# Two-layer graph network on one core: list places dropped and weighted on ScalarE after layer 0, and more room before the last steps

## The chip, the cores and the metric

The kernel runs on one core of one Trainium2 chip. The core has five engines that run side by side, each on its own queue of instructions in a fixed order: TensorE (PE, with its weight loads PEld), VectorE (DVE), ScalarE (ACT), GpSimd (POOL) and SyncE (SP, which here only issues DMAs). They meet through semaphores. The metric is the device time of one execution in microseconds (us); less is better.

## What is computed

Sixteen graphs of 1024 nodes with 64 channels each go through two layers. Layer 0 is a dense, degree-normalised neighbour sum of a normalised input. Layer 1 takes, for every node and channel, a weighted sum of three quantiles over the node's neighbours, after some neighbours have been removed, and puts the result through a two-layer MLP.

```python
def reference(x, adj, nodemask, W1, b1, W2, b2):
    h = relu(layernorm(x))                                  # layer 0
    x = x + matmul(adj / clip(sum(adj, 2), 1), h)
    h = relu(layernorm(x))                                  # layer 1
    valid = dilate_adj(adj, nodemask) > 0                   # with the node itself
    agg = 0
    for tau, wt in ((.25, .25), (.5, .5), (.75, .25)):
        agg += wt * quantile(h over the valid neighbours, tau)   # linear interpolation
    y = relu((h + agg) @ W1 + b1) @ W2 + b2
    return x + y * nodemask

def dilate_adj(adj, mask):
    # a node with m > 10 neighbours removes each (m+1)//2-th of them; an edge that
    # either end removes is gone
    ...
```

The adjacency matrices are sparse (a few hundred neighbours for the first nodes of a graph, a handful for most), so layer 1 works on lists of neighbours.

## The kernel before

**Layer 0** goes graph by graph. SP loads 128 rows of adjacency at a time (`at`); PE transposes them and multiplies them with the normalised input; ScalarE takes signs, VectorE turns the signs into lists of neighbour numbers (`rec`). At the end of a graph its normalised rows go to a table in DRAM (`tab`), and POOL scatters a row per node (`srt<-row`) into one of four sorted tables, one for each group of four graphs, so that nodes with lists of similar length stand together.

**Layer 1** works on jobs (class `Job`, from line 797). A job takes T blocks of 128 nodes whose lists have at most n-1 places. There are ten jobs of short lists for each of the four groups (`gat`, up to 15 places), and four jobs of long lists (88, 31, 24 and 20 places, tiles with an l in front). Before a group's jobs run, `group` (line 1027) prepares them: `recs` and `nodes_i` are made, POOL reads one block of adjacency rows (`gat_rows`), two corrections are scattered to the table (`tab<-drop`). `long_lists` (line 1145) prepares a long list in the same way, with a read of adjacency rows into `lat`. Of a job:

- `run` (808): POOL gathers, one indirect DMA for each place and block, from the table into `places` (four buffers) or `lplaces`. A last wait (831) hands over to VectorE.
- `sort` (844): VectorE finds which places have been removed (`rem`, `gone`), how many are left (`ok`, `valid`), the quantile positions (`q`) and three weights for each place (`wu`, finished by ScalarE). It adds a huge number to the places that are gone (876 to 880). Then come the steps of a sorting network between `places` and `other` (in PSUM) or `long_other`; the weights are added up (`w`) and multiplied with the sorted places into `prod`, or in place for a long list (938 to 946).
- `layers` (965): PE adds up and transposes, ScalarE copies (`ot`), PE multiplies, ScalarE applies the relu (`hid`), PE multiplies, VectorE adds the residual (`y`, 1013), and POOL scatters the T blocks of y to the output (`out_dram`, 1022).

**What sets the order.** The kernel is written as streams (Python generators) that a planner, class `Plan`, merges. A stream yields the engine that it needs next, a function for the time at which its operands are ready or a buffer is free, and sometimes a rank. The planner keeps a clock for each engine by prices that stand in the code, always continues the stream that can begin first, and at equal times the one of lower rank. The order in which VectorE and POOL execute is the order in which the planner emitted their instructions; at run time an engine stands before its next instruction until that one's semaphores are there, and everything behind it stands too. `at(tile)` is the planned time at which a tile is ready, `room(name, bufs)` the planned time at which the oldest of so many buffers is free. The constants SLACK and LOOSE (lines 213 and 214) are planned microseconds added to `at`, so that an instruction is placed somewhat after its operands are planned to be ready. `later` (837) gives the rank of a job's steps: ahead of others while POOL has few gathers left to issue (`progress["ahead"] < AHEAD`), behind them otherwise. `progress["batches"] == B` means that layer 0 of all sixteen graphs has been emitted.

Of the kernel before, what the change touches and what calls it, by code (L numbers as in the profile page):

```python
# [9 lines left out]
F32 = mybir.dt.float32  # L10
BF = mybir.dt.bfloat16
# [3 lines left out]
AF = mybir.ActivationFunctionType  # L15
# [196 lines left out]
AHEAD = 16  # L212
SLACK = 2.0
LOOSE = 7.0


class Timed:
# [146 lines left out]
def list_path(ctx, tc, x, adj, nodemask, w1, b1, w2, b2, out, go):  # L364
# [434 lines left out]
    class Job:  # L799
# [8 lines left out]
        def run(self):  # L808
            n, T, pool, short = self.n, self.T, self.pool, self.short

            since = []
            own = () if short else (lambda rank: self.rank,)
            pace = lambda: since[0] + 1.3 * len(since) if not short else 0.0
            yield "POOL", lambda: max(
                at(self.idx), room(self.name, self.bufs), room("S", 4) if short else 0.0
            ), *own
            A = self.A = new(pool, [P, n, T, W], F32, self.name, self.bufs, users=1)
            progress["ahead"] += T * (n - 1)
            if short:
                mine = self.S  # L820
                self.S = new(pool, [P, T, C], F32, "S", 4, users=1)
                nc.sync.dma_start(self.S, mine[:, :, :C])
                self.residual = mine[:, :, X1:R0]
            for t in range(T):
                for k in range(n - 1):
                    if t or k:
                        yield "POOL", pace, *own
                    since.append(since[0] if since else plan.clock["POOL"])
                    gather(A[:, k + 1, t, :], self.table, self.idx[:, t, k:k + 1])
                    progress["ahead"] -= 1  # L830
            yield "DVE", lambda: max(
                at(A, self.S) + SLACK, room("prod", 2) if short else 0.0,
                room("other" if short else "long_other", 1),
            ), self.later
            yield from self.sort()

        def later(self, rank):

            return rank - 900 if progress["ahead"] < AHEAD else rank + 2000

        def urgent(self):
            return -1000 if progress["ahead"] < AHEAD else 5000

        def sort(self):
# [5 lines left out]
                rem, A[:, 1:, :, C:],  # L850
                self.node.unsqueeze(1).unsqueeze(3).to_broadcast([P, n - 1, T, 2]), OP.is_equal,
            )
            gone = new(pool, [P, n - 1, T], F32, name + "gone", bufs)
            nc.vector.tensor_tensor(gone, rem[:, :, :, 0], rem[:, :, :, 1], OP.max)
            ok = new(pool, [P, n - 1, T], F32, name + "ok", bufs)
            nc.vector.scalar_tensor_tensor(
# [10 lines left out]
                q, taus.unsqueeze(2).to_broadcast([P, K, T]),  # L867
                valid.unsqueeze(1).to_broadcast([P, K, T]), OP.mult,
            )
            u = new(pool, [P, K, count, T], F32, name + "wu", 1)  # L870
            nc.vector.tensor_tensor(
                u, col_f[:, :count].unsqueeze(1).unsqueeze(3).to_broadcast([P, K, count, T]),
                q.unsqueeze(2).to_broadcast([P, K, count, T]), OP.subtract,
            )
            vals = A[:, 1:, :, :].rearrange("p k t w -> p (k t) w")[:, :, :C]
            nc.vector.scalar_tensor_tensor(
                vals,
                gone.rearrange("p k t -> p (k t)").unsqueeze(2).to_broadcast([P, (n - 1) * T, C]),
                HUGE, vals, op0=OP.mult, op1=OP.add,
            )  # L880
            if short:
                Bt = new(ps_o, [P, 3 * HALF], F32, "other", 1, users=1)
                other = Bt[:, :n * T * C].rearrange("p (k t c) -> p k t c", k=n, t=T)
            else:
                other = Bt = new(pool, [P, n, T, C], F32, "long_other", 1, users=1)
            yield "ACT", lambda: at(u) + SLACK
            nc.scalar.activation(u, u, AF.Abs)
            nc.scalar.activation(u, u, AF.Relu, bias=wt0, scale=-QUANTILES[0][1])

            def places(copy, run, shift=0):  # L890
                first, d1, n1, d2, n2 = run
# [36 lines left out]
            w = new(pool, [P, count, T], F32, name + "w", bufs)  # L928
            nc.vector.tensor_tensor(w, u[:, 0, :, :], u[:, 1, :, :], OP.add)
            nc.vector.scalar_tensor_tensor(w, u[:, 2, :, :], 2.0, w, op0=OP.mult, op1=OP.add)  # L930

            total = max(count + 1, 4)
            prod = None
            if short:
                prod = new(pool, [P, T, total, C], F32, "prod", 2, users=1)
                if count + 1 < total:
                    nc.vector.memset(prod[:, :, count + 1:, :], 0.0)
            for copy in range(2):
                for run in runs_of([k for k in range(count) if copies[k] == copy]):
                    first, step, number = run[:3]  # L940
                    sl = slice(first, first + step * (number - 1) + 1, step)
                    src = places(copy, run)
                    nc.vector.tensor_tensor(
                        prod[:, :, sl, :].rearrange("p t k c -> p k t c") if short else src, src,
                        w[:, sl, :].unsqueeze(3).to_broadcast([P, number, T, C]), OP.mult,
                    )
            if short:
                free(A)
                free(Bt)
                yield "ACT", lambda: at(S)  # L950
                nc.scalar.copy(prod[:, :, count, :], S[:, :, :C])
                free(S)

                terms = [
                    [prod[:, t, k:min(k + 2, total), :].rearrange("p k c -> p (k c)")
                     for k in (0, *range(4, total, 2), 2)]
                    for t in range(T)
                ]
                plan.add(self.layers(terms, [prod]), self.urgent)
            else:  # L960
                terms = [[places(copies[k], (k, 1, 1, 1, 1))[:, 0, 0, :] for k in range(count)]
                         + [S[:, 0, :C]]]
                plan.add(self.layers(terms, [A, Bt]), -1000)

        def layers(self, terms, sources):

            T, R = self.T, terms[0][0].shape[1]
            yield "PE", lambda: max(at(*sources) + LOOSE, room("y", 5), room("pt", 2))
            y = new(mlp, [P, T, CO], F32, "y", 5, users=1)
            x1 = y  # L970
            if self.short:
                nc.sync.dma_start(x1, self.residual)
# [2 lines left out]
            for t0 in range(0, T, 4):  # L975
                ts = range(t0, min(t0 + 4, T))
                M = len(ts) * P
                if t0:
                    yield "PE", lambda: room("pt", 2)
                pt = new(ps_t, [P, HALF], F32, "pt", 2, users=1)  # L980
                for i, t in enumerate(ts):
                    for k, term in enumerate(terms[t]):
                        nc.tensor.matmul(
                            pt[:term.shape[1], i * P:(i + 1) * P], term, ident,
                            start=(k == 0), stop=(k == len(terms[t]) - 1),
                        )
                if t0 + 4 >= T:
                    for tile_ in sources:
                        free(tile_)
                yield "ACT", lambda: max(at(pt) + SLACK, room("ot", 2))  # L990
                ot = new(mlp, [2 * C, HALF], F32, "ot", 2)
                nc.scalar.copy(ot[:R, :M], pt[:R, :M])
                free(pt)
                yield "PE", lambda: max(at(ot) + SLACK, room("ps_small", 3))
                ph = new(ps_s, [P, HALF], F32, "ps_small", 3, users=1)
                nc.tensor.matmul(ph[:, :M], w1_sb[:R, :], ot[:R, :M], start=True, stop=True)
                yield "ACT", lambda: max(at(ph) + SLACK, room("hid", 2))
                hid = new(mlp, [H, HALF], F32, "hid", 2)
                nc.scalar.activation(hid[:, :M], ph[:, :M], AF.Relu, bias=b1_sb)
                free(ph)  # L1000
                yield "PE", lambda: max(at(hid) + SLACK, room("ps_small", 3))
                py = new(ps_s, [P, HALF], F32, "ps_small", 3, users=1)
                pv = py[:, :len(ts) * CO].rearrange("p (t c) -> p t c", c=CO)
                nc.tensor.matmul(
                    py[:, :len(ts) * CO], ones_f[:1, :], b2_sb[:, :len(ts) * CO],
                    start=True, stop=False,
                )
                for i, t in enumerate(ts):
                    nc.tensor.matmul(
                        pv[:, i, :], hid[:, i * P:(i + 1) * P], w2_sb, start=False,  # L1010
                        stop=(i == len(ts) - 1),
                    )
                yield "DVE", lambda: at(py) + LOOSE
                for i, t in enumerate(ts):
                    nc.vector.scalar_tensor_tensor(
                        y[:, t, :], pv[:, i, :], self.mask[:, t:t + 1], x1[:, t, :],
                        op0=OP.mult, op1=OP.add,
                    )
                free(py)

            for t in range(T):
                yield "POOL", lambda: at(y) + LOOSE
                scatter(out_rows, y[:, t, :], self.nodes_i[:, t:t + 1], scatters)
            free(y)
            progress["jobs"][self.g] += 1
# [1 line left out]
    def group(g):  # L1027
# [22 lines left out]
        gather(full, adj_rows, nodes_i[:, 0:1])  # L1050
        yield "DVE", always

        found = new(grp, [P, NTAU, 8 * NSEG], BF, "gfound", 1)
        nc.vector.tensor_scalar(found, lists, 0.0, None, op0=OP.is_gt)
        m = tiny.tile([P, NTAU], F32, name="gm")
        nc.vector.tensor_reduce(m, found, AX.X, OP.add)
# [52 lines left out]
        nc.vector.scalar_tensor_tensor(  # L1109
            full, col_f, node[:, 0:1], full, op0=OP.not_equal, op1=OP.mult  # L1110
        )
        nb = new(grp, [P, N], BF, "nb", 1)
        nc.vector.tensor_scalar(nb, full, 0.0, None, op0=OP.is_gt)
        cum = full
        nc.vector.tensor_tensor_scan(cum, nb, zeros, 0.0, op0=OP.add, op1=OP.add)
# [421 lines left out]
```

## Time and profile before

| | |
|---|---|
| median of 3 runs | 1572.41 us (1570.78 to 1575.34) |
| profiled execution | 1573.65 us, its span 1571.9 us |
| mean granted TensorE clock in it | 0.687 |
| last row scatter of layer 0 begins | 826.16 us |
| last gather begins | 1537.34 us |
| last store of y begins | 1563.06 us |

The page cuts the span into 40 slices; a digit is the busy share of a slice in tenths:

```profile
DVE  6767899997997699999556897659779889878962
ACT  7889888346565536664630000000000010000001
POOL 0222238665578767568676666587777678566775
```

Layer 0 ends a little after the middle. Behind it ScalarE has almost nothing to do, while VectorE sorts and POOL gathers. All instructions that the planner records carry line 225, that of its helper, so groups are told apart by their tiles: `places<-tab,idx` is a gather, `out_dram<-y,nodes_i` a store, `places<-gone,places` the addition that drops places, `prod<-places,w` a product with weights. These rows have places (p) x elements, the count, the busy time, the mean of one in ns and the idle time before it:

```profile
L225 POOL DMA_INDIRECT places<-tab,idx x496 | 507.4, 1023 | 159.9 <-issue 146.1
L225 POOL DMA_INDIRECT lplaces<-tab,lidx x163 | 173.7, 1066 | 51.0 <-issue 47.9
L225 POOL DMA_INDIRECT out_dram<-y,nodes_i x124 | 130.6, 1053 | 99.2 <-DVE y L225 53.6
L225 DVE SCALAR_TENSOR_TENSOR y<-ps_small,recs,y 128x64 f32<-128x64 f32 x124 | 28.0, 276 | 81.0 <-PE ps_small L225 80.9
```

"issue" is time in which the engine waited for nothing that the profile shows.

### The profile page before, as it was taken

The page shows a single profiled execution, that of the slowest core. Times are in us where ns is not written, and L with a number is a line of the kernel's source. Part 1 is how long each engine was busy: PE and PEld are TensorE (multiplying, and loading weights), DVE is VectorE, ACT ScalarE, POOL GpSimd, SP SyncE. Part 2 cuts the span into 40 slices and gives each one's busy share as a digit, 9 for nine tenths or more (in the row PEclk, how much of TensorE's full clock was granted, in tenths as well). Part 3 has the DMA queues.
Part 4 walks back from the last instruction along what each step waited for, and adds up shares of the span by engine and source line. Part 5 has one row for each costly group of instructions (what it writes and reads, how often), then busy time and mean ns, then how long its engine had stood idle before and what let it go on. Part 6 is the DMA issues. An engine that isn't in the chain of part 4 may idle for free. (4 is left out here: it accounts for less than half of the span.)

```text
span 1571.9 us, 14933 instructions
## 1 busy us (share of the span) xinstructions
PE 744.4 (47%) x3192; PEld 465.3 (30%) x3192; DVE 1260.4 (80%) x4174; ACT 578.5 (37%) x1746; POOL 989.3 (63%) x1149
## 2 busy tenths in 40 slices
PE   5787776365756754855880001200021367124355
PEld 2334443133343532532450001100021156023244
DVE  6767899997997699999556897659779889878962
ACT  7889888346565536664630000000000010000001
POOL 0222238665578767568676666587777678566775
PEclk8888998686977866976895555555555567555657
DMA  5455666244542433652222111111121111111110
GB/s 161 134 149 167 175 198 188 71 124 100 177 121 60 120 106 108 165 149 66 75 51 66 41 38 36 33 27 23 25 41 34 24 28 24 28 31 36 31 29 21
DMA packets 135530, 128.95 MB, mean 82 GB/s; under 512 B 100696, under 2 KB 103384, under 8 KB 135432
## 3 DMA queue, kind: packets, MB, share of 16 engines
q1 hardware_dynamic: 102696, 86.46, 19.7%
q0 software_dynamic: 32736, 41.47, 11.6%
q8 instruction: 27, 0.44, 0.1%
q14 instruction: 71, 0.58, 0.1%
HBM read 108.57 MB, written 19.28 MB: 81 GB/s over the span
## 5 line engine op out<-in xcount | busy, mean ns | idle before, releaser
L225 POOL DMA_INDIRECT places<-tab,idx x496 | 507.4, 1023 | 159.9 <-issue 146.1
L225 PE MATMUL pt<-ident,prod 128*128 128x128 f32 (+1 forms) x736 | 168.0, 395 | 627.5 <-DVE prod L225 586.7
L225 PEld LDWEIGHTS pt<-ident,prod 128*128 128x128 f32 (+1 forms) x736 | 136.6, 273 | 659.6 <-DVE prod L225 406.0
L225 PE MATMUL ps_small<-att,h 128*65 128x512 f32 x512 | 260.1, 657 | 44.1 <-ACT h L225 28.3
L225 POOL DMA_INDIRECT srt<-row,to x128 | 129.5, 1012 | 176.2 <-ACT row L225 154.8
L225 POOL DMA_INDIRECT lplaces<-tab,lidx x163 | 173.7, 1066 | 51.0 <-issue 47.9
L225 PE MATMUL pt<-ident,at 128*128 128x128 f32 x1024 | 167.3, 308 | 80.7 <-ACT att L225 68.9
L225 POOL DMA_INDIRECT out_dram<-y,nodes_i x124 | 130.6, 1053 | 99.2 <-DVE y L225 53.6
L225 DVE MAX8 rec<-sg 128x8 f16<-128x256 f16 x512 | 180.1, 414 | 4.4
L225 PEld LDWEIGHTS pt<-ident,at 128*128 128x128 f32 x1024 | 129.4, 157 | 126.2 <-ACT att L225 93.7
L225 ACT ACTIVATE sg<-at 128x1024 f16<-128x1024 f32 x128 | 134.9, 1054 | 54.2 <-DMA at<-in_adj_dram 34.6
L225 ACT COPY att<-pt 128x512 f32<-128x512 f32 x256 | 141.5, 582 | 22.7 <-PE pt L225 20.7
L225 ACT COPY ot<-pt 128x128 f32<-128x128 f32 (+3 forms) x56 | 22.2, 401 | 308.9 <-PE pt L225 308.6
L225 ACT ACTIVATE wu<-wu 128x39 f32<-128x39 f32 (+9 forms) x40 | 9.4, 235 | 337.7 <-DVE wu L225 337.6
L225 PEld LDWEIGHTS ps_small<-att,h 128*65 128x65 f32 x512 | 75.8, 154 | 184.3 <-issue 128.5
L225 DVE TENSOR_TENSOR sg<-sg,keyed 128x1024 f16<-128x1024 f16 x128 | 87.6, 684 | 37.3 <-ACT sg L225 37.2
L225 DVE SCALAR_TENSOR_TENSOR y<-ps_small,recs,y 128x64 f32<-128x64 f32 x124 | 28.0, 276 | 81.0 <-PE ps_small L225 80.9
L225 DVE TENSOR_TENSOR other<-places,other 128x64 f32<-128x64 f32 (+6 forms) x204 | 69.7, 342 | 5.6
L225 DVE TENSOR_TENSOR places<-places,other 128x64 f32<-128x64 f32 (+2 forms) x208 | 62.4, 309 | 4.9
L225 DVE TENSOR_TENSOR long_other<-lplaces 128x512 f32<-128x512 f32 (+5 forms) x124 | 63.9, 553 | 0.4
L225 DVE TENSOR_TENSOR lplaces<-long_other 128x512 f32<-128x512 f32 (+7 forms) x116 | 61.4, 567 | 0.1
L225 DVE TENSOR_TENSOR places<-other,places 128x128 f32<-128x128 f32 (+5 forms) x160 | 54.9, 343 | 3.5
(206 smaller groups left out, 1516.1 us busy)
## 6 DMA issues: line engine op xcount, KB each, us to landing
at<-in_adj_dram SPq DMA_DIRECT2D x128, 512.0 KB
places<-tab,idx POOLq DMA_INDIRECT x496
tab<-row SPq DMA_DIRECT2D x16, 264.0 KB
xt<-in_x_dram SPq DMA_DIRECT2D x16, 256.0 KB
lplaces<-tab,lidx POOLq DMA_INDIRECT x163
recs<-srt SPq DMA_DIRECT2D x4, 544.0 KB
srt<-row,to POOLq DMA_INDIRECT x128
out_dram<-y,nodes_i POOLq DMA_INDIRECT x124
```

What stands on the lines that cost most here:

```text
L225: ins = getattr(self._engine, op)(*args, **kwargs)
```

## The change

Five things are changed, all in the planner's streams:

1. For a job whose preparation is emitted once layer 0 is done, the huge number is no longer added by one VectorE instruction: ScalarE multiplies `gone` by it and adds it as a per-partition bias, one activation for each place and block.
2. For such a job ScalarE also multiplies with the weights, one activation for each place and block: for a short list those places whose sorted value ends in `places` (copy 0), for a long list all.
3. The preparation up to `wu` is separated from the sort. It waits for its operands and for the buffers of `gone` and `wu` (two of each for short lists), by a rank of its own (`soon`); the sort then waits for the places, for `prod` and for `other`.
4. y is placed LATE = 14 instead of LOOSE = 7 planned microseconds after its matmuls, the store 14 instead of 7 after y, and y has six buffers instead of five.
5. In `group`, `found` and `nb` share a buffer.

```diff
+LATE = 14.0
...
             yield "DVE", lambda: max(
-                at(A, self.S) + SLACK, room("prod", 2) if short else 0.0,
-                room("other" if short else "long_other", 1),
-            ), self.later
+                at(A, self.S) + SLACK,
+                *(room(("" if short else "l") + name, 2 if short else 1) for name in ("gone", "wu")),
+            ), self.soon
             yield from self.sort()
...
+        def soon(self, rank):
+
+            return rank - (950 if progress["ahead"] < AHEAD else -1900)
...
-            vals = A[:, 1:, :, :].rearrange("p k t w -> p (k t) w")[:, :, :C]
-            nc.vector.scalar_tensor_tensor(
-                vals,
-                gone.rearrange("p k t -> p (k t)").unsqueeze(2).to_broadcast([P, (n - 1) * T, C]),
-                HUGE, vals, op0=OP.mult, op1=OP.add,
-            )
+
+            helped = progress["batches"] == B
+            if helped:
+                yield "ACT", lambda: at(gone) + SLACK
+                nc.scalar.mul(gone, gone, HUGE)
+                for t in range(T):
+                    for k in range(1, n):
+                        if (t or k > 1) and k % 4 == 1:
+                            yield "ACT", always
+                        val = A[:, k, t, :C]
+                        nc.scalar.activation(val, val, AF.Identity, bias=gone[:, k - 1, t:t + 1])
+            else:
...
+            free(gone)
+            yield "ACT", lambda: at(u) + SLACK
+            nc.scalar.activation(u, u, AF.Abs)
+            nc.scalar.activation(u, u, AF.Relu, bias=wt0, scale=-QUANTILES[0][1])
+            yield "DVE", lambda: max(
+                at(A) + SLACK if helped else 0.0, room("prod", 2) if short else 0.0,
+                room("other" if short else "long_other", 1),
+            ), self.later
...
-            for copy in range(2):
-                for run in runs_of([k for k in range(count) if copies[k] == copy]):
+
+            helped = progress["batches"] == B
+            for copy in (1, 0):
+                mine = [k for k in range(count) if copies[k] == copy]
+                if helped and (copy == 0 or not short):
+                    yield "ACT", lambda: at(w) + SLACK
+                    for e, k in enumerate(mine):
+                        if e and e % 4 == 0:
+                            yield "ACT", always
+                        for t in range(T):
+                            src = places(copy, (k, 1, 1, 1, 1))[:, 0, t, :]
+                            nc.scalar.activation(
+                                prod[:, t, k, :] if short else src, src, AF.Copy,
+                                scale=w[:, k, t:t + 1],
+                            )
+                    continue
+                for run in runs_of(mine):
...
-            yield "PE", lambda: max(at(*sources) + LOOSE, room("y", 5), room("pt", 2))
-            y = new(mlp, [P, T, CO], F32, "y", 5, users=1)
+            yield "PE", lambda: max(at(*sources) + LOOSE, room("y", 6), room("pt", 2))
+            y = new(mlp, [P, T, CO], F32, "y", 6, users=1)
...
-                yield "DVE", lambda: at(py) + LOOSE
+                yield "DVE", lambda: at(py) + LATE
...
-                yield "POOL", lambda: at(y) + LOOSE
+                yield "POOL", lambda: at(y) + LATE
...
-        found = new(grp, [P, NTAU, 8 * NSEG], BF, "gfound", 1)
+        found = new(grp, [P, N], BF, "gfound", 1).rearrange("p (t e) -> p t e", t=NTAU)
...
-        nb = new(grp, [P, N], BF, "nb", 1)
+        nb = new(grp, [P, N], BF, "gfound", 1)
```

More of the change, by code (lines that the diff above doesn't have):

```diff
@@ L852, in sort @@
             )
-            gone = new(pool, [P, n - 1, T], F32, name + "gone", bufs)
+            gone = new(pool, [P, n - 1, T], F32, name + "gone", bufs, users=1)
             nc.vector.tensor_tensor(gone, rem[:, :, :, 0], rem[:, :, :, 1], OP.max)
@@ L869, in sort @@
             )
-            u = new(pool, [P, K, count, T], F32, name + "wu", 1)
+            u = new(pool, [P, K, count, T], F32, name + "wu", bufs, users=1)
             nc.vector.tensor_tensor(
@@ L874, in sort @@
             )
-            vals = A[:, 1:, :, :].rearrange("p k t w -> p (k t) w")[:, :, :C]
-            nc.vector.scalar_tensor_tensor(
-                vals,
-                gone.rearrange("p k t -> p (k t)").unsqueeze(2).to_broadcast([P, (n - 1) * T, C]),
-                HUGE, vals, op0=OP.mult, op1=OP.add,
-            )
+            helped = progress["batches"] == B
[9 more added lines that the diff above has]
+            else:
+                vals = A[:, 1:, :, :].rearrange("p k t w -> p (k t) w")[:, :, :C]
+                nc.vector.scalar_tensor_tensor(
+                    vals,
+                    gone.rearrange("p k t -> p (k t)").unsqueeze(2).to_broadcast(
+                        [P, (n - 1) * T, C]
+                    ),
+                    HUGE, vals, op0=OP.mult, op1=OP.add,
+                )
[7 more added lines that the diff above has]
+            ), self.later
             if short:
@@ L885, in sort @@
                 other = Bt = new(pool, [P, n, T, C], F32, "long_other", 1, users=1)
-            yield "ACT", lambda: at(u) + SLACK
-            nc.scalar.activation(u, u, AF.Abs)
-            nc.scalar.activation(u, u, AF.Relu, bias=wt0, scale=-QUANTILES[0][1])
             def places(copy, run, shift=0):
@@ L930, in sort @@
             nc.vector.scalar_tensor_tensor(w, u[:, 2, :, :], 2.0, w, op0=OP.mult, op1=OP.add)
+            free(u)
             total = max(count + 1, 4)
@@ L937, in sort @@
                     nc.vector.memset(prod[:, :, count + 1:, :], 0.0)
-            for copy in range(2):
-                for run in runs_of([k for k in range(count) if copies[k] == copy]):
+            helped = progress["batches"] == B
[11 more added lines that the diff above has]
+                                scale=w[:, k, t:t + 1],
+                            )
+                    continue
+                for run in runs_of(mine):
                     first, step, number = run[:3]
@@ L949, in sort @@
                 free(Bt)
-                yield "ACT", lambda: at(S)
+                if not helped:
+                    yield "ACT", lambda: at(S)
                 nc.scalar.copy(prod[:, :, count, :], S[:, :, :C])
```

## The prediction

> **What bounds the kernel now.** I read the page first (engines, forty slices), then busy time by stretch, then the waits of each engine from 780 us on, then the timeline round the longest of them. All sums are against the profiled execution: 1573.65 us, of which 1571.9 is the span; the median of the runs shown is 1572.41, so a figure for one stands for the other within 0.1%.
>
> ```profile
> PE 744.4 (47%) x3192; PEld 465.3 (30%) x3192; DVE 1260.4 (80%) x4174; ACT 578.5 (37%) x1746; POOL 989.3 (63%) x1149
> ...
> 826.00:1572.00 746.00, 191.29 (x887) 149.52 (x886) 578.27 (x1863) 45.03 (x128) 523.21 (x554) 0.56 0.16 32
> ...
> POOL places L225 <- issue: 76.9, 249, 1.3
> POOL lplaces L225 <- issue: 47.9, 157, 0.3
> POOL out_dram L225 <- DVE y L225: 41.3, 12, 10.8
> ...
> POOL gat_rows L225 <- DVE lkeys L225: 9.9, 1, 9.9
> POOL lat L225 <- DVE other L225: 6.7, 2, 6.4
> ...
> DVE y L225 <- PE ps_small L225: 80.9, 18, 9.4
> DVE lrem L225 <- DMA lplaces<-tab,lidx: 21.7, 1, 21.7
> ```
>
> The page makes VectorE (DVE, 80%) look like the bound. The stretch after layer 0 (its last row scatter ends at 827 us) says otherwise: of 746 us VectorE works 578, ScalarE (ACT) 45, GpSimd (POOL) 523. But a POOL gather of 0.95 us is followed by 0.30 of issue each time, so 523 busy us are some 665 occupied ones. POOL issues 489 DMAs from 827 to 1564; the waits longer than the issue gap add to 73 us; (737 - 73)/489 = 1.36 us each. No gather waits for a buffer there: "places <- issue" means POOL waits for nothing but itself. So the tail is POOL's queue, plus 73 us in which its head is not ready: 47 are stores waiting for y, 9.6 the read of adjacency rows for the last group (gat_rows), 9.6 those of the long lists (lat), the rest small. VectorE in turn loses 80.9 us standing before y. The timeline shows how the two hang together:
>
> ```profile
> 1401.49 0.94 POOL L225 DMA_INDIRECT places<-tab,idx  x1 [0.30 <-issue]
> ...
> 1407.17 0.37 ACT L225 COPY ot<-pt 128x256 f32<-128x256 f32 x1 [1.54 <-PE pt L225]
> ...
> 1409.92 0.47 DVE L225 SCALAR_TENSOR_TENSOR y<-ps_small,recs,y 128x64 f32<-128x64 f32 x2 [4.48 <-PE ps_small L225]
> 1410.48 0.98 POOL L225 DMA_INDIRECT out_dram<-y,nodes_i  x1 [8.05 <-DVE y L225]
> ...
> 1413.09 0.98 POOL L225 DMA_INDIRECT places<-tab,idx  x1 [0.30 <-issue]
> ```
>
> The MLP of one list is late by 4.48 us; VectorE stands before y in its fixed order, POOL stands before the store for 8.05, while gathers that lacked nothing stand behind it.
>
> **What the Trainium skill says.** "ScalarE: Activation LUTs", section "Table sets: the hidden batching unit", gives an activation with a pointer as bias about 280 ns + 0.833 ns per element, and 93 ns of overlap back to back: for 64 elements 333 and 240 ns. The trace agrees: the 128x32 activation with a pointer bias lasts 318 ns (307 by the page) and follows its like after 211 (214). "Perfetto Trace Analysis", "Per-instruction lifecycle", says that the wait for a semaphore lies outside an instruction's slice; so waits are read here from idle time before a slice. "DMA: Bandwidth & Descriptors", "Anatomy of one DMA — SWDGE (gpsimd) path", says that waits happen on the issuing sequencer and not in the DMA engines: a store that isn't ready holds all later gathers. The 8.05 us above are that.
>
> **The change part by part**, with the counts from the order of instructions in both built programs.
>
> 1. *Dropped places on ScalarE.* 24 of the 44 jobs (groups 2 and 3, the long lists) lose their VectorE add: 30 us (the dearest row: lplaces<-lgone 128x5632, 6.02 us). ScalarE gains 411 activations of 64 elements and 24 multiplications.
> 2. *Weights on ScalarE.* 249 more activations; VectorE loses 18 us of products. With part 1 VectorE's work, at the traced durations, falls from 1261 to 1214 us. ScalarE's 660 activations at 0.24 us are 158 us in a stretch where it works 45. VectorE was not the bound, so the 47 us by themselves bring nothing.
> 3. *What parts 1 and 2 add as waits.* A sort now waits for ScalarE. A list of 20 places takes 4.8 us, the 88-place list 21 us where VectorE took 6.0. Where other VectorE work lies between a list's preparation and its sort (the long lists' steps, mostly) this is covered. In the built order it is not in about five places: three before the last group's preparation (about 2.5 us each, 7 together), the 88-place list (15 after overlap with its first sorting layer), and the first list of group 3 behind 12 weights (3). Behind each stands all VectorE work, and behind that the stores and buffers POOL wants.
> 4. *LATE = 14 for the last step and the stores, six y buffers.* y is placed 7 planned us later behind its matmuls, and the store another 7 behind y. The 18 waits for y are 4.5 us on average and 9.4 at most, the stores' 10.8 at most; 14 us in all cover each of them, so 43 of the 47 us go. The last four at the kernel's end stay: nothing is left to put before them.
> 5. *Earlier preparation (soon; two buffers of gone and wu), one buffer for gfound and nb.* It moves work only. VectorE's work before layer 0's last index is 664 us for 667, so layer 0 ends where it did, at about 800; the 29 us of store waits that POOL has before 826 bring nothing, since its next scatters wait for layer 0. But positions move. Layer 0's last scatter is POOL's 434th DMA instead of the 442nd: it ends about 7.5 us earlier (the store before it needs a y right behind layer 0's last index, 801.5; six gathers and eight scatters make 819.6), and leaves eight more DMAs, 8 x 1.36 = 10.9. The last group's preparation stands 86 us of VectorE work behind layer 0 instead of 39. POOL reaches gat_rows at about 889, VectorE gives its index at about 905 (824 when the long lists' rows are there, 5 for the first adjacency read, 70 of work, 7 of part 3): 16 us instead of 9.6. The three lat waits fall from 9.6 to about 6.
>
> Then the long gathers end later (601st DMA against the 578th), so the 88-place list starts at about 1068 instead of 1039. From there VectorE has 367 us of work and POOL 330 DMAs x 1.36 = 449. With 15 us for the first drop I compared both at each store and at the three gathers that now wait for a buffer's release: POOL comes 10 to 16 us after VectorE from its 719th to its 832nd DMA, 20 and more after. VectorE's new idle time in that stretch (leftover y waits and drops) is bounded by 0 and by the 50 it had there before; I take 15, of which 3 reach POOL.
>
> Sum: -43 (stores) -7.5 +10.9 (positions) +6.5 (gat_rows) -3.5 (lat) +3 (VectorE late) = -33.6. Adding up POOL's queue stretch by stretch instead, with 1.27 us for stores and 1.32 per DMA for the part before the long gathers, gives -44, because the slow gathers are not evenly spread. I take -37: 1573.65 - 37 = about 1536 us.
>
> **Rivals.**
> - *A: the forecast.* 1536, own range 1515 to 1555.
> - *B: VectorE becomes the bound of the middle.* For it: the margins of 10 to 16 us are thin, and the built order has three gathers waiting for ScalarE's release of a buffer where before none did. Against it: VectorE keeps over 100 us idle. With 35 us idle in the stretch, 20 more reach POOL: 1558 (1552 to 1567).
> - *C: more goes than I count.* All waits before gat_rows and lat go too, and layer 0 ends 10 us earlier (VectorE idles 23 us in its last 50): 1573.65 - 37 - 22 - 4 = about 1510.
> - *D: slower. ScalarE is too slow for its place.* Place: the stretch from the 88-place list to POOL's 832nd DMA, where some 205 activations stand before sorts with little cover. If each took 0.44 instead of 0.24 us (the dearest 64-element row, with two pointers, shows 0.43 long and 0.33 from start to start) that is 41 us, all beyond the margin in use, and the gain is gone; at 0.5 us it is 53, and the time about 1590. Against it: the row with one pointer.
> - *E: it doesn't do what it says.* The built program shows the 660 activations and the moved stores; that they bring nothing because real waits drift from planned ones leaves 1569 to 1578.
>
> **How the numbers follow.** A 0.62, B 0.17, C 0.07, D 0.09, E 0.05. The predicted time is A's, 1536. The range reaches over C's near half and B: 1508 to 1566. A measurement of this kernel can tell some 0.3% (5 us) from no change: faster takes A, B, C, and a little of E, 0.86; same 0.05; slower 0.09.
>
> **What would show it.** In the changed profile: stores waiting for y in the tail under 10 us (part 4; above 25 it is wrong); VectorE's waits before y under 30 of 80.9; VectorE busy 1214 and ScalarE about 735; drops 240 ns from start to start; a gat_rows wait near 16; sorts waiting for ScalarE, some 30 us in all. The forecast fails if gathers wait for places, or if layer 0's last scatter ends after 835.

## The result and the profile after

The changed kernel takes 1554.92 us (median of 4 runs, 1552.33 to 1557.26) where the kernel before took 1571.6: a ratio of 0.989, interval 0.9866 to 0.9914. That is 17 us less; the forecast was 37. The page of the changed kernel, engines and three of the rows of slices:

```profile
PE 752.3 (48%) x3192; PEld 467.4 (30%) x3192; DVE 1215.7 (78%) x4125; ACT 735.3 (47%) x2430; POOL 966.3 (62%) x1151
...
DVE  6767899997899479899854988960499998899751
ACT  7899888346365483665632031000500347424352
POOL 0222228674676757356777737577787777777764
```

ScalarE now works in the second half of the span, and VectorE has lost 45 us, as forecast. The groups of gathers, stores, last steps and activations (count | busy, mean ns | idle before, and what ended it):

```profile
L226 POOL DMA_INDIRECT places<-tab,idx x496 | 497.1, 1002 | 156.2 <-issue 142.9
L226 POOL DMA_INDIRECT lplaces<-tab,lidx x163 | 165.3, 1014 | 50.1 <-issue 49.0
L226 POOL DMA_INDIRECT out_dram<-y,nodes_i x124 | 123.8, 999 | 53.6 <-DVE y L226 22.0
L226 ACT ACTIVATE places<-places,gone 128x64 f32<-128x64 f32 x248 | 61.6, 334 | 0.4
L226 DVE SCALAR_TENSOR_TENSOR y<-ps_small,recs,y 128x64 f32<-128x64 f32 x124 | 27.8, 275 | 25.7 <-PE ps_small L226 25.5
```

Two things are to be seen. The idle time before stores fell from 99.2 to 53.6 us. And the gathers and stores themselves became shorter: their mean fell from 1023, 1066 and 1053 ns to 1002, 1014 and 999. The second was in no line of the forecast. The waits after layer 0 (engine, tile, waited for, us, times, longest):

```profile
DVE lrem L226 <- DMA lplaces<-tab,lidx: 44.5, 1, 44.5
DVE other L226 <- ACT places L226: 26.0, 6, 8.0
DVE long_other L226 <- ACT lplaces L226: 25.8, 9, 7.1
DVE y L226 <- PE ps_small L226: 25.5, 8, 6.3
POOL gat_rows L226 <- DVE places L226: 21.7, 1, 21.7
POOL out_dram L226 <- DVE y L226: 14.9, 3, 8.3
```

No gather waits for a buffer. The last row scatter of layer 0, with the index (`to`) of graph 12 before it, first in the kernel before and then in the changed one (start, duration, engine, operation, what ended its idle time):

```profile
585.11 0.17 DVE L225 SCALAR_TENSOR_TENSOR to<-low,pos 128x8 int32<-128x8 int32 x1
...
826.16 0.96 POOL L225 DMA_INDIRECT srt<-row,to  x1 [0.19 <-ACT hid L225]
```

```profile
614.89 0.20 DVE L226 SCALAR_TENSOR_TENSOR to<-low,pos 128x8 int32<-128x8 int32 x1
...
842.50 0.96 POOL L226 DMA_INDIRECT srt<-row,to  x1 [0.19 <-issue]
```

Layer 0 ends 16 us later, where the forecast had it 7.5 earlier. Here is the hole.

**One account for all kernels.** After the last row scatter the end is POOL's queue. Its DMAs are summed in four terms: where the last scatter ends; a base, which is what remains; stalls (idle before an instruction over the 0.3 us of issue, where it is over 0.5); and the excess of slow DMAs (what those over 1.15 us last beyond 0.96). Divided by the count, the base is 1.267 to 1.272 us per DMA in each of these seven, so the other three terms are what differs. Profiled executions, us:

| kernel | last scatter ends | DMAs after it | base | stalls | excess | last DMA ends |
|---|---|---|---|---|---|---|
| before | 827.1 | 489 | 622.0 | 72.8 | 42.1 | 1564.0 |
| changed | 843.5 | 497 | 629.5 | 50.2 | 22.8 | 1545.9 |
| e15, room alone | 818.3 | 498 | 631.0 | 45.6 | 47.6 | 1542.6 |
| e6, nothing on ScalarE | 842.8 | 497 | 630.8 | 44.1 | 48.5 | 1566.2 |
| e14, as e6, gone in PSUM | 845.0 | 497 | 630.2 | 49.1 | 34.7 | 1559.0 |
| e5, layer 0 as before | 828.7 | 483 | 613.4 | 61.5 | 23.5 | 1527.1 |
| e13, early preparation after layer 0 only | 830.5 | 490 | 620.8 | 47.9 | 26.0 | 1525.2 |

From before to changed: +16.4 (layer 0) +7.5 (base, with eight more DMAs) -22.6 (stalls) -19.3 (excess) = -18.0.

### The profile page after: what moved, and what is told of

It is laid out like the page before. It is cut to its first block, busy times and chain, and to the rows that moved or that the text cites. A ratio compares the mean times of both kernels' runs of the same rounds, so it can differ in the third digit from the quotient of the medians.

```text
span 1553.6 us, 15675 instructions
## 1 busy us (share of the span) xinstructions
PE 752.3 (48%) x3192; PEld 467.4 (30%) x3192; DVE 1215.7 (78%) x4125; ACT 735.3 (47%) x2430; POOL 966.3 (62%) x1151
## 5 line engine op out<-in xcount | busy, mean ns | idle before, releaser
L226 POOL DMA_INDIRECT places<-tab,idx x496 | 497.1, 1002 | 156.2 <-issue 142.9
L226 POOL DMA_INDIRECT srt<-row,to x128 | 134.0, 1047 | 216.1 <-ACT row L226 187.7
L226 PE MATMUL pt<-ident,at 128*128 128x128 f32 x1024 | 161.1, 301 | 73.4 <-ACT att L226 55.4
L226 POOL DMA_INDIRECT lplaces<-tab,lidx x163 | 165.3, 1014 | 50.1 <-issue 49.0
L226 PEld LDWEIGHTS pt<-ident,at 128*128 128x128 f32 x1024 | 125.1, 153 | 123.1 <-ACT att L226 80.3
L226 POOL DMA_INDIRECT out_dram<-y,nodes_i x124 | 123.8, 999 | 53.6 <-DVE y L226 22.0
L226 ACT ACTIVATE gone<-gone 128x15 f32<-128x15 f32 (+9 forms) x20 | 4.1, 205 | 183.8 <-DVE ok L226 183.7
L226 PE MATMUL ps_small<-ot,w_sb 128*128 128x128 f32 (+3 forms) x112 | 51.3, 550 | 40.0 <-ACT ot L226 19.4
L226 ACT ACTIVATE prod<-places,w 128x64 f32<-128x64 f32 x122 | 30.9, 334 | 82.7 <-DVE w L226 82.7
L226 PE MATMUL ps_small<-w_sb,hid 128*128 128x64 f32 x256 | 53.5, 353 | 18.7 <-ACT hid L226 18.3
```

The source lines that it names most:

```text
L226: ins = getattr(self._engine, op)(*args, **kwargs)
```

## The experiments

Five runs (e5, e6, e13, e14, e15) took place on chips where the kernel before takes 1570 to 1572 us. Ten others fell to chips where it takes 1909 to 1927; they are told last, since their times can't be set against 1572. The theories in the expectations: L, the change lost part of its gain because layer 0 ends later; S, because sorts wait for ScalarE; V, what gains is VectorE's work taken away. L1 lays layer 0's delay on the early preparation, L2 on the room for last steps and stores.

**e5: layer 0 as before.** Until layer 0 is emitted, preparation and sort stay one step and the room stays at 7.

```diff
+            early = progress["batches"] < B
+            if early:
+                yield "DVE", lambda: max(
+                    at(A, self.S) + SLACK, room("prod", 2) if short else 0.0,
+                    room("other" if short else "long_other", 1),
+                ), self.later
+            else:
+                yield "DVE", ..., self.soon
...
-                yield "DVE", lambda: at(py) + LATE
+                yield "DVE", lambda: at(py) + (LATE if progress["batches"] == B else LOOSE)
...
-                yield "POOL", lambda: at(y) + LATE
+                yield "POOL", lambda: at(y) + (LATE if progress["batches"] == B else LOOSE)
```

> The changed kernel with two of its edits bound to the time after layer 0: until the last graph's places are sorted, a list is prepared as in the kernel before (one step, right ahead of its sort), and the last step and the stores keep 7 us of room; after it both are as changed. The changed kernel took 0.989 of the kernel before, with layer 0's last row scatter ending at 843.5 us (827.1 before). L (the middle graphs' indices come later in layer 0, and GpSimd carries that to layer 0's end): the index of graph 12 comes near 585 us again (614.9 changed), layer 0's last scatter ends at 820 to 830, and the whole is 0.968 to 0.980 of the kernel before, 1522 to 1541 us. S (ScalarE's drops ate the gain, layer 0 is no part of it): 0.984 to 0.994, since the tail is the same. The last scatter at 838 or later with a time near 1555 would leave L wrong.

Measured: 1538.26 us, 0.9785 (0.9764 to 0.9806). Graph 12's index comes at 583.6 us and the last scatter ends at 828.7. L holds, S (0.984 to 0.994) doesn't: with ScalarE's help unchanged, the missing part of the gain came back once layer 0 was left alone.

**e6: nothing on ScalarE**, all else as changed.

```diff
-            helped = progress["batches"] == B
+            helped = False
```

> The changed kernel with the dropped places and weights of all lists on VectorE (no activation place by place), everything else as changed: layer 0 is in the same order. L: layer 0's last scatter ends at 840 to 847 us, as in the changed kernel. S (ScalarE's drops cost the forecast's missing 17 us): 0.975 to 0.984 of the kernel before. V (taking 47 us of work off VectorE is what gained): 0.997 to 1.01. Neither (the drops are about even, since VectorE has slack): 0.985 to 0.996. VectorE is to be busy some 1262 us and ScalarE some 580; the sorts' waits for ScalarE's drops, 52 us in the changed kernel, are to be gone.

Measured: 1576.25 us, 1.0027 (1.0011 to 1.0043). The last scatter ends at 842.8, so L's place is right again. But the time is V's: without ScalarE the rest of the change brings nothing, and ScalarE's share is 21 us (1576.25 - 1554.92). This contradicts the forecast, which said that 47 us less on VectorE bring nothing by themselves. The table shows where they come from: stalls are even a little lower without ScalarE (44.1 against 50.2), and the excess is 25.7 us higher. So it seems not to be VectorE's time that counts, but what VectorE's instructions do to POOL's. The timeline of e6 at the largest of them:

```profile
1092.25 0.95 POOL L226 DMA_INDIRECT lplaces<-tab,lidx  x1 [0.30 <-issue]
...
1092.90 6.02 DVE L226 SCALAR_TENSOR_TENSOR lplaces<-lgone,lplaces 128x5632 f32<-128x5632 f32 x1
...
1093.50 6.23 POOL L226 DMA_INDIRECT lplaces<-tab,lidx  x1 [0.30 <-issue]
1098.95 1.91 DVE L226 TENSOR_TENSOR long_other<-lplaces 128x512 f32<-128x512 f32 x3
1100.04 1.03 POOL L226 DMA_INDIRECT lplaces<-tab,lidx  x1 [0.31 <-issue]
```

A gather begun 0.6 us into the add lasts 6.23 us instead of 0.95 and ends 0.8 us after the add does. Both operands of the add lie in SBUF. The Trainium skill, "SBUF — State Buffer", section "Who interferes with whom", states that a VectorE instruction with two SBUF inputs contends with a GpSimd instruction that reads SBUF, because the second input comes through a read interface that the two engines share; it calls the shared ports an exclusive lock. The lines agree. An indirect DMA's indices lie in SBUF here; that this is the read in question isn't shown by any run. With each slow DMA put down to the VectorE instruction that it overlaps longest, 11 DMAs with 11.8 us of excess stood beside adds of dropped places in e6. From this came theory P (the shared read, not VectorE's time), and its test.

**e14: the same adds with one operand in PSUM.** After layer 0 the flags `gone` are written to PSUM. VectorE does the same instructions on as many elements. The flags take one of the three `ps_small` buffers that the MLP uses too, and the preparation also waits for one of these to be free.

```diff
+            if progress["batches"] == B:
+                gone_t = new(ps_s, [P, HALF], F32, "ps_small", 3, users=1)
+                gone = gone_t[:, :(n - 1) * T].rearrange("p (k t) -> p k t", t=T)
+            else:
+                gone = gone_t = new(pool, [P, n - 1, T], F32, name + "gone", bufs, users=1)
```

> The kernel of e7_gone_psum and e10_gone_psum (all drops on VectorE, the flags gone in PSUM after layer 0), for its time where the kernel before takes some 1570 us. P: excess beside the adds of dropped places under 2 us (11.8 in e6_no_help), the sum after layer 0 35 to 39 instead of 48.5, the time 1560 to 1569 (0.993 to 0.9985 of before; e6_no_help 1.0027). V: 1571 to 1581.

Measured: 1567.07 us, 0.9972 (0.996 to 0.9984), in P's range; V's began at 1571. VectorE is busy 1259.3 us (1259.2 in e6). The same add in the timeline:

```profile
1095.02 6.02 DVE L226 SCALAR_TENSOR_TENSOR lplaces<-ps_small,lplaces 128x5632 f32<-128x5632 f32 x1
...
1095.75 0.94 POOL L226 DMA_INDIRECT lplaces<-tab,lidx  x1 [0.30 <-issue]
1097.00 0.95 POOL L226 DMA_INDIRECT lplaces<-tab,lidx  x1 [0.30 <-issue]
1098.25 0.95 POOL L226 DMA_INDIRECT lplaces<-tab,lidx  x1 [0.30 <-issue]
1099.51 0.94 POOL L226 DMA_INDIRECT lplaces<-tab,lidx  x1 [0.30 <-issue]
```

It lasts 6.02 us as before, and POOL issues one gather after another beside it. None of the DMAs over 1.15 us stands beside an add of dropped places any more; the sum falls from 48.5 to 34.7 (P said 35 to 39), of which 5.0 go back into stalls and 2.2 into a later layer 0. So for the adds it is shown that the place of the operand counts, and not VectorE's time. Beside the products with weights, the rest of what ScalarE takes, e6 has the same picture:

```profile
1360.94 4.55 DVE L226 TENSOR_TENSOR lplaces<-lplaces,lw 128x4224 f32<-128x4224 f32 x1
1361.36 4.96 POOL L226 DMA_INDIRECT places<-tab,idx  x1 [0.30 <-issue]
```

Five DMAs with 7.0 us of excess stand beside products there, none in the changed kernel; but no run moved a product's operands. Adds and products are 18.8 of the 25.7 us between e6 and the changed kernel. The rest lies mostly beside steps of the long sorts, which VectorE does in both; why fewer DMAs are slow there isn't shown.

**e15: the room alone.** The kernel before with LATE = 14, six y buffers and the shared buffer; no early preparation, nothing on ScalarE.

```diff
-                yield "DVE", lambda: at(py) + LOOSE
+                yield "DVE", lambda: at(py) + LATE
...
-                yield "POOL", lambda: at(y) + LOOSE
+                yield "POOL", lambda: at(y) + LATE
```

> The kernel of e9_late_alone and e12_late_alone (the room for last steps and stores, six y buffers and the shared buffer on the kernel before), where that takes some 1570 us. L2 (the room delays layer 0): last scatter at 835 or later; L1: 818 to 830. Part 4 of the forecast: the stores' waits after layer 0 fall from 47 to under 20 us; excess of GpSimd's DMAs 42 to 50 us as before; 0.985 to 0.996 of before. 0.997 or more: the room is of no use by itself.

Measured: 1550.44 us, 0.9857 (0.9834 to 0.988): 4.5 us less than the whole change. The runs of the two don't overlap (at most 1552.1 against at least 1552.33), the intervals of their ratios do. Its index of graph 12 and last scatter, by the timeline, and its store waits after layer 0:

```profile
544.56 0.17 DVE L226 SCALAR_TENSOR_TENSOR to<-low,pos 128x8 int32<-128x8 int32 x1
...
817.35 0.96 POOL L226 DMA_INDIRECT srt<-row,to  x1 [0.19 <-issue]
```

```profile
DVE y L226 <- PE ps_small L226: 25.6, 11, 6.8
...
POOL out_dram L226 <- DVE y L226: 12.5, 1, 12.5
```

L2 falls: with the room everywhere, layer 0 ends 8.8 us earlier, as the forecast had put it (7.5). The stores' stalls fall from 47.0 to 12.2, and the excess stays (47.6). e6 differs from e15 by the early preparation and its buffers (and by the order of the two groups of products), and is 26 us slower (1576.25 against 1550.44); in the table, 24.5 us of it are the later end of layer 0.

**e13: early preparation after layer 0 only**, the room everywhere (the first hunk of e5 without the other two).

> The changed kernel with the early preparation of lists only once layer 0 is done; 14 us of room everywhere. On a chip on which the kernel before takes some 1572 us. L1 (the early preparation alone delays the middle graphs): index of graph 12 at 575 to 590 us, layer 0's last scatter at 820 to 830, 0.974 to 0.983 of before. L2 (the room for stores delays them): last scatter at 835 or later, 0.983 to 0.99.

Measured: 1536.76 us, 0.9785 (0.9758 to 0.9812).

```profile
575.42 0.17 DVE L226 SCALAR_TENSOR_TENSOR to<-low,pos 128x8 int32<-128x8 int32 x1
...
829.55 0.96 POOL L226 DMA_INDIRECT srt<-row,to  x1 [0.19 <-issue]
```

L1 holds for the index and the time; the last scatter ends at 830.5, half a microsecond beyond its range, and 12 us later than in e15. About 10 of these are order: POOL has issued 441 DMAs by then in e13, 433 in e15, and has eight fewer left. Why this order came out, with graph 12's index 31 us later than in e15, isn't shown. e13 and e5 are 18 and 17 us below the changed kernel, and beat both kernels; between the two no difference is shown. What e13 still waits for after layer 0, besides the issue gaps:

```profile
POOL places L226 <- ACT gone L226: 14.6, 1, 14.6
POOL out_dram L226 <- DVE y L226: 11.4, 5, 5.5
POOL gat_rows L226 <- DVE lkeys L226: 10.7, 1, 10.7
```

The first is a gather that waits for ScalarE to let go of a buffer: it shows here and in e5 (15.2 us), the two in which POOL's queue ends earliest.

**Runs on other chips.** e1 to e4 were the first test of L, S and V: the room alone, nothing on ScalarE, the changed kernel with LATE = 7, and the kernel of e5.

> The kernel before with the later y, the later stores and six y buffers alone (and the shared buffer of group). Theory L (the change lost part of its gain because the middle graphs of layer 0 end later, and POOL with them): the moved stores are the whole gain, the work moved to ScalarE none, so this runs within 8 us of the changed kernel, 1547 to 1563, with under 15 us of stores waiting for y after layer 0. Theory S (ScalarE's drops cost the gain, since sorts wait 52 us for them): without them it is clearly faster than the changed kernel, 1540 or less. Theory V (taking 47 us off VectorE is what gains): 1566 or more.

> The changed kernel with drops and weights back on VectorE; its order within layer 0 is instruction for instruction that of the changed kernel. Theory L: within 8 us of the changed kernel, 1547 to 1563, the last row scatter of layer 0 near 843 us as there. Theory S: 1540 or less. Theory V: 1570 or more, with gathers or stores waiting for VectorE in the middle.

> The changed kernel with LATE at 7, so the moved stores and y undone; ScalarE's help stays. Theory L: the stores' waits of some 40 us come back after layer 0 and it runs 1580 to 1605. If instead the later stores themselves delay layer 0: 1560 or less.

> The changed kernel, but within layer 0 the early preparation and LATE are off (both begin once layer 0 is done), so that layer 0's list indices stand behind about the same VectorE work as before (487 us for the twelfth graph; 485 before, 499 in the change). Theory L: the twelfth graph is scattered by about 630 us, not 661, the last graph by about 828, not 843, and the kernel gains what the tail gains: 1518 to 1535. Theory S or V: no better than the changed kernel, 1550 to 1560.

Measured: 1932.31 (1.0116, 1.0057 to 1.0175), 1947.42 (1.0248), 1958.56 (1.0254) and 1931.42 us (1.0129), with the kernel before at 1908.79. All four are slower than it, on a chip where all kernels wait for something else as well (last section), so none of the theories is told by them. e7 (the kernel of e14), e8 (that of e13) and e9 (that of e15) met the same with before at 1926.94: 2018.07 (1.0488), 2017.31 (1.0481) and 1980.26 us (1.0276). One thing can be read from e7 without its time:

> The kernel with all drops and weights on VectorE (e6_no_help) with one difference, once layer 0 is done: the flags gone, one of the two operands of the wide add, lie in PSUM instead of SBUF. VectorE does the same instructions on as many elements. P (a GpSimd DMA that is issued beside a VectorE instruction with two SBUF operands stands until that instruction ends, and this, not VectorE's time, is what ScalarE's help took away): in e6_no_help GpSimd's DMAs after layer 0 last 48.5 us more than 0.96 us each, 11.8 of them beside the adds of the dropped places; these 11.8 go to under 2, the sum to 35 to 39, and the time from 1576 to 1560 to 1569. V (what counts is the 47 us of VectorE's work): the excess beside the adds stays near 12 and the time at 1571 to 1581.

No slow DMA of e7 stands beside an add of dropped places; in e2, with gone in SBUF, 11 do, with 11.7 us. e10 to e12 were these three kernels again, at 1.0522, 1.0497 and 1.0301 of 1925.14 us, and add only that e10, too, shows none. LATE = 7 by itself (e3) was not run where before takes 1572, nor was the changed kernel run where it takes 1909 or more.

## Why the forecast was right in sign and too large

Its sum, term by term (profiled executions, us):

| term | forecast | measured |
|---|---|---|
| stores' waits after layer 0 (part 4) | -43 | -30.9 |
| end of layer 0's last scatter (part 5) | -7.5 | +16.4 |
| eight more DMAs after it (base) | +10.9 | +7.5 |
| gat_rows | +6.5 | +11.8 |
| lat | -3.5 | -0.5 |
| VectorE late, other stalls | +3 | -3.0 |
| slow DMAs | not in the sum | -19.3 |
| sum | -33.6 (taken as -37) | -18.0 |

- **The step that failed is part 5**, "so layer 0 ends where it did, at about 800", and the 7.5 us put on it. The last scatter ended at 843.5, beyond the 835 that the forecast itself had named as a sign of being wrong. The early preparation "moves work only", it said, and the proof was VectorE's work before the last index, 664 us for 667. That number came true, and the index came at 804.6. But POOL's last scatter isn't released by it alone: POOL walks its own queue there, and its stalls stem from the middle graphs. Graph 12's index came at 614.9 instead of 585.1. 15 of these 30 us are VectorE's work that now stood ahead of it (501 us instead of 486), the rest is time in which VectorE stood longer, mostly waiting for ScalarE's signs (12.6 us before, 22.4 changed, between graph 9's index and graph 12's). The first row scatters of graph 12, before and changed:

```profile
619.71 1.26 POOL L225 DMA_INDIRECT srt<-row,to  x1 [3.57 <-ACT row L225]
```

```profile
650.79 0.99 POOL L226 DMA_INDIRECT srt<-row,to  x1 [12.89 <-ACT row L226]
```

From 400 us to the last scatter POOL's stalls, counted as in the table of kernels, are 68.0 us instead of 40.8. Those before row scatters rose from 3.3 to 34.5, while those before stores fell. Less some 10 us for the eight DMAs that now come later, that is the 16 us. The planned order by itself gives the work ahead of graph 12 (485 us before, 499 changed); only the end of the row was read. e6 against e15, and e13 against the changed kernel, show that the early preparation does it, and e15 that the room alone brings the forecast's earlier end. In e6 VectorE has 500 us of work before graph 12's index, in e15 457. The instructions that stand there in addition last 49 us if each is counted in full, and 29 of these are steps of sorts of lists: the lists were not only prepared early, their sorts then came earlier too.
- **Parts 1 and 2** have their sizes right and their worth wrong. VectorE 1215.7 (1214), ScalarE 735.3 (735), 334 ns for an activation, where the Trainium skill, "ScalarE: Activation LUTs", section "What ACT_TABLE_LOAD costs", gives 333. But "the 47 us by themselves bring nothing" is wrong: taking the wide adds and products off VectorE shortened POOL's DMAs. The kernel before showed it; the forecast noticed "slow gathers" and carried them through as given:

```profile
1041.13 6.02 DVE L225 SCALAR_TENSOR_TENSOR lplaces<-lgone,lplaces 128x5632 f32<-128x5632 f32 x1
1041.84 6.12 POOL L225 DMA_INDIRECT lplaces<-tab,lidx  x1 [0.30 <-issue]
```

- **Part 3** was low: 52 us of sorts waiting for ScalarE, not 30, the longest 8.0 instead of 15. It cost little, since no gather waited for a buffer and the later stores had room.
- **Part 4** had the mechanism right and its worth 12 us too high: VectorE's waits before y fell to 25.5 (under 30 forecast). Of the stores' stalls 16.1 are left instead of 4, and 13.4 of these are two stores at the end of the kernel, which stood 3.8 there before. e15 gives the part's own worth: 21 us of the time.
- **The rivals.** B's time, 1558 (by its own terms, 1536 and 20 more, 1556), lies nearest, but its mechanism isn't there: no gather waits for a buffer after layer 0. D is excluded by the activations, 23 of which follow one another in 5.59 us in the changed kernel's timeline, 0.243 each; E by e15 and e6 against the changed kernel. Two misses of opposite sign, +20 for layer 0 with the eight DMAs (3.4 forecast, 23.9 measured) and -19 for the excess, make the result look closer to the forecast than its working was.

```profile
1094.70 5.59 ACT L226 ACTIVATE lplaces<-lplaces,lgone 128x64 f32<-128x64 f32 x23
```

Put on one after the other, on chips where the kernel before takes 1570 to 1572 us, the room is worth -21 us (before to e15), the early preparation +26 (to e6), ScalarE's help -21 (to the changed kernel). With the early preparation held back from layer 0, the kernel comes to 1536.76 us; that this is the forecast number is chance, since the terms are others.

## What to carry to other kernels

When one engine's fixed queue ends last, write its time as start, count times base, stalls and excess of slow instructions, and ask of each edit what it does to each of the four; a busy engine beside it can cost through its operands without ever being waited for. Where an edit reorders a stage, compare the marks of the whole stage, not its last: a queue carries a delay in the middle to the end if it has no slack after it. Bind an edit that is meant for one stage to that stage. And name the chips on which a gain was measured: e5's and e13's kernels, 2% faster here, were 1.3% and 5% slower than the kernel before on the others (e4; e8 and e11).

## What the runs showed of the hardware

In these traces a wide VectorE add with two SBUF operands holds a GpSimd indirect DMA that begins during it (6.23 us for 0.95); with one operand in PSUM, at the same length, it doesn't. In e6, 18 DMAs begin at least 0.2 us before the end of an add of dropped places. 16 of them end 0.81 to 0.88 us after the add does, however much of it was left; the other two, begun within 0.03 us of the add's start, take 0.94 and 0.95. In e14 there are 22, and none takes over 0.99. Short sorts, whose second tile lies in PSUM, have little of it; the long lists' sorts, with both tiles in SBUF, make most of the excess that the best kernels keep (17.5 of 23.5 us in e5, 19.0 of 26.0 in e13).

The chips differ more than the kernels. On three of them the kernel before took 1909 to 1927 us instead of 1572, VectorE busy for as long (1266.2 us in e9, 1261.5 in e15, the same kernel) and the mean granted TensorE clock lower (0.641 and 0.688). Lines from the timeline of e9, in the sort of the 88-place list:

```profile
1361.29 0.69 DVE L226 TENSOR_TENSOR lplaces<-lplaces 128x512 f32<-128x512 f32 x1 [3.05 <-issue]
...
1361.89 0.70 DVE L226 TENSOR_TENSOR lplaces<-lplaces 128x512 f32<-128x512 f32 x1
...
1365.49 0.55 DVE L226 TENSOR_TENSOR lplaces<-lplaces 128x384 f32<-128x384 f32 x1 [2.90 <-issue]
...
1369.69 0.71 DVE L226 TENSOR_TENSOR long_other<-long_other 128x512 f32<-128x512 f32 x1 [3.05 <-issue]
```

Every 4.2 us VectorE stands for 3 with nothing that the profile shows it waiting for. The group of the 124 steps long_other<-lplaces has 29.4 us of idle time before it in e9, 0.3 in e15. The cause stays open. The kernel before shows the slowness too, so it doesn't come from the change; but on such chips all of the change's parts that ran there came out slower than the kernel before.
